# A convolution moved from layer 1's beginning into layer 0's last image, and a reordered first image

## The chip, the cores and the metric

The kernel runs on one core of one Trainium2 chip. The metric is the device time of one execution in microseconds; three executions of the kernel before took 8372.44, 8380.8 and 8384.7 us, so its median is 8380.8 us. The engines are called as in the profile: PE (matrix multiply), PEld (its weight load), DVE (vector), ACT (activation), POOL (GpSimd), SP (the queue that issues all DMAs here).

## The reference

Two layers work on 16 images of 128 channels and 56 x 56 pixels, in float32. Layer 0 is an attention block over windows, layer 1 a convolution, a state-space scan and a group norm. Cut to what matters here:

```python
# layer 0, for each image
x = x + dwconv3x3(x, pos_w, pos_b)                 # "position": 9 taps per channel
y = layernorm(x) over channels
q, k, v = split(y @ qkv_w + qkv_b)                 # 49 windows of 64 pixels
idx = top4(mean(q per window) @ mean(k per window).T)
o = softmax(q k[idx]) v[idx]  per window, 4 heads
o = o + dwconv5x5(v)                               # "lepe": 25 taps per channel
x = x + o @ wo + b
x = x + gelu(layernorm(x) @ w1 + b1) @ w2 + b2     # "MLP"
# layer 1, for each image
y = conv3x3(x, conv_w) + conv_b                    # full 128 x 128 channels, 9 taps
out = mamba(y as sequences of 8 tokens of 16)
return x + silu(groupnorm(out))
```

## The kernel before

**Layer 0** (`layer0`, L163) holds one image in a padded tile `xpad` (58 x 58 per channel, channels on the 128 partitions) and cuts it into seven blocks of eight lines, 448 pixels each, which are called rows here. For the first image everything up to the routing is done in one stretch ahead of the loop: for each row, DVE computes the nine position taps (`begin`, L246, then eight times L252), PE centres the row over the channels (L268, into the PSUM bank `g0`), ACT squares it, PE averages (L276), ACT makes the inverse deviation (L280, L281), DVE multiplies (`windows`, L289) and sums, and PE projects it to q, k and v (L303, into the banks `pvt`, `po` and `g0`), from where ACT copies them out. The next row's centring uses the bank `g0` too. Then the sums of all windows are routed (`sums`, `route`), the first five windows are gathered (`gather`, four DMAs a window on SP's queue), POOL lays three rows of v into padded tiles (`surround`), DVE does 56 slots of the local convolution (`convolve_on(56)`, which are 44 taps, as the slots of two rows alternate and the odd ones of the first 25 are empty), and POOL does the first two rows of image 1 (`beside`: a start, and seven products and sums, L262 and L264; the ninth tap is DVE's).

The loop then takes 49 windows per image (`step`). A step t issues on PE the scores of window t, the attention product of window t-2, the transposes of the weights of t-1 and, in even columns, of the values; DVE takes the largest score (L364) ahead of ACT's exponentials, which free the scores' bank for the next step, and works on taps of the local convolution; POOL scales the weights. The column c = t mod 7 decides which further matmul comes in (`piece`): in columns 1 to 3 the output product, the centring and the variance of the row before (they use `pvt` and `g0`), in columns 0, 1, 4, 5 and 6 those of the next image. In the last image there is no next one, and these latter places stay empty. `mlp` (L604) follows with the MLP of seven rows, whose results are stored to DRAM (`x1`) by one DMA per row; row 6 of an image is done within the next image, and for the last image behind the loop. At t = 46 and 48 the image after next is loaded into `xpad`.

Inside `layer0` the order of every engine and of the DMA queue is the order in which the Python code issues (`_chain` adds a dependence from each instruction to the one before it on its engine). The preparation ahead of it (constants, their scaling) is left to the scheduler. SP's queue keeps at most eight DMAs under way: the ninth waits for the first one's semaphore.

**Layer 1** (`layer1`, L713) loads its own weights once layer 0's memory is free, folds two of them with factors on DVE (L762), clears a padded tile `x1pad`, loads image 0 into it from `x1`, and convolves its seven rows one after the other into one bank (`convolve`, L782: nine taps of a 128 x 128 x 448 matmul, two passes each, then two or three ACT copies, L797). Then it loads image 1 and begins the loop over groups; each group is a row of an image. The convolution of the next image's rows is spread over the loop, so only image 0's stands ahead of it. The first group begins with the transposes of `y` (`sequences`, L830), the inner projection (L838), the rate (L851), and so on to the first DVE instruction of the scan (L937).

Of the kernel before, what the change touches and what calls it, by code (L numbers as in the profile page):

```python
# [10 lines left out]
F32 = mybir.dt.float32  # L11
U32 = mybir.dt.uint32
AF = mybir.ActivationFunctionType
# [4 lines left out]
P = 128  # L18
H = W = 56
HW = H * W  # L20
# [3 lines left out]
BLK = 448  # L24
# [114 lines left out]
def _load(nc, pool, ap, name):  # L139
    t = pool.tile(list(ap.shape), F32, tag=name, name=name)  # L140
    nc.sync.dma_start(t, ap)
    return t
# [16 lines left out]
        last[i.engine] = i.name  # L159


@with_exitstack
def layer0(ctx: ExitStack, tc: tile.TileContext, x, t, x1):  # L163

# [17 lines left out]
    w6 = ctx.enter_context(tc.tile_pool(name="l0w6", bufs=AHEAD + 1))  # L184
    banks = ctx.enter_context(tc.tile_pool(name="l0p", bufs=1, space=PSUM))

    pos = _load(nc, cst, t["a_pos"], "pos")
    lep = _load(nc, cst, t["a_lepe"], "lep")
    wqkv = _load(nc, cst, t["a_qkv"], "wqkv")
# [4 lines left out]
    ident = _load(nc, cst, t["k_ident"], "ident0")  # L194
    mean = _load(nc, cst, t["k_mean"], "mean")
    centre = _load(nc, cst, t["k_centre"], "centre")
    pos_b, ln1_g, ln1_b, lepe_b, wo_b, ln2_g, ln2_b, mlp_b2 = (vec[:, i : i + 1] for i in range(8))

    def bank(name):
# [21 lines left out]
    zero = cst.tile([P, 1], F32, tag="zero0", name="zero0")  # L221
    nc.vector.memset(zero, 0.0)

    xpad = cst.tile([P, H + 2, W + 2], F32, tag="xpad", name="xpad")
    nc.gpsimd.memset(xpad, 0.0)
    vpads = [cst.tile([P, 12, W + 4], F32, tag=f"vpad{k}", name=f"vpad{k}") for k in range(3)]
    for v in vpads:
        nc.gpsimd.memset(v, 0.0)
# [293 lines left out]
    def step(im, nxt, t):  # L522
        r, c = divmod(t, WIN)
        b = im["b"]
        n = f"{b}_{t}"
        out, row = (im, r - 1) if r else (images[b - 1], NBLK - 1)
        old, new = r > 0 or b > 0, nxt is not None
        if t + AHEAD < NW:
            gather(im, t + AHEAD)
        if t in (46, 48) and b + 2 < NB:  # L530
            load(b + 2, t // 2 - 23)

        if c < 3 and new and r:
            keep(nxt, r - 1, c)
        if c == 2 and old:
            residual(out, row)
        if c == 3 and old:
            squared(n)
        if c == 4 and old:
            deviation(n)  # L540
        if c == 5 and new:
            squared(n)
        if c == 6 and new:
            deviation(n)
        if t > 0 or b == 0:
            open_step(im, t)
        if t > 1:
            attend(im, t - 2)
        if c == 1 and r:
            collect(im, r - 1)  # L550
        if c == 4 and old:
            second(out, row)
        if c == 6 and new:
            windows(nxt, r)
        convolve_on(TAPS[c] - 1)
        if new:
            if t == 1:
                position(nxt, 1, (8,))
            if t in (10, 19, 28, 37, 45):
                position(nxt, 2 + (10, 19, 28, 37, 45).index(t), (8,))  # L560
            count = len(OPS)
            for k in range(5 * count * t // 45, min(5 * count * (t + 1) // 45, 5 * count)):
                beside(nxt, 2 + k // count, k % count)
        exponentials(im, t)
        inverse(im, t)
        if t in (1, 8, 17, 27):
            surround(im, 3 + (1, 8, 17, 27).index(t))
        if t in (36, 44) and new:
            surround(nxt, (t - 36) // 8)
        weights(im, t)  # L570
        if c == 1 and new and r:
            project(g0, 2)
        waits = c in (1, 4, 6)
        if not waits:
            piece(im, nxt, out, row, c, r)
        if t > 0:
            transpose_weights(im, t - 1)
            keep_weights(im, t - 1)
        if c % 2 == 0:
            transpose_values(im, t)  # L580
            keep_values(im, t)
        convolve_on(1)
        if waits:
            piece(im, nxt, out, row, c, r)

    def piece(im, nxt, out, row, c, r):

        old, new = r > 0 or im["b"] > 0, nxt is not None
        if c == 0 and new and r:
            project(g0, 1)  # L590
        if c == 1 and old:
            project_out(pvt)
        if c == 2 and old:
            centred(g0, out, row)
        if c == 3 and old:
            variance(pvt)
        if c == 4 and new:
            centred(g0, nxt, r)
        if c == 5 and new:
            variance(pvt)  # L600
        if c == 6 and new:
            project(g0, 0)

    def mlp(im, nxt):  # L604

# [8 lines left out]
        for m in range(count + 1):  # L614
# [10 lines left out]
            if m == 0:  # L625
                transpose_weights(im, NW - 1)
                keep_weights(im, NW - 1)
                if nxt:
                    for s in (1, 2):
                        project(g0, s)  # L630
                        keep(nxt, last, s)
                convolve_on(10)
                if nxt:
                    surround(nxt, 2)
            if m < count:
                expand(*blocks[m], 2)
            if m == 1 and nxt:
# [15 lines left out]
        _act_set(tc, EXP_LN)  # L653

    start = len(nc.cur_bb.bb.instructions)
    load(0, 0)
    load(0, 1)
    _act_set(tc, EXP_LN)
    im = images[0]
    begin(im, 0, nc.vector)  # L660
    position(im, 0, range(1, 9))
    for i in range(NBLK):
        n = f"0_{i}"
        centred(g0, im, i)
        squared(n)
        variance(ptt)
        deviation(n)
        if i + 1 < NBLK:
            begin(im, i + 1, nc.vector)
            position(im, i + 1, range(1, 9))  # L670
        windows(im, i)
        for s, at in enumerate((pvt, po, g0)):
            project(at, s)
            keep(im, i, s)
    if NB > 1:
# [3 lines left out]
    route(im)  # L679
    for w in range(AHEAD):  # L680
        gather(im, w)
    for r in range(3):
        surround(im, r)
    convolve_on(56)
    if NB > 1:
        for i in range(2):
            for k in range(len(OPS)):
# [22 lines left out]


@with_exitstack
def layer1(ctx: ExitStack, tc: tile.TileContext, x1, t, out):  # L713

# [23 lines left out]
    ps_x = ctx.enter_context(tc.tile_pool(name="l1px", bufs=1, space=PSUM))  # L740
    ps_q = ctx.enter_context(tc.tile_pool(name="l1pq", bufs=1, space=PSUM))

    conv = _load(nc, cst, t["b_conv"], "conv")
    wx = _load(nc, cst, t["b_wx"], "wx")
    wz = _load(nc, cst, t["b_wz"], "wz")
    wv = _load(nc, cst, t["b_wv"], "wv")
# [1 line left out]
    adec = _load(nc, cst, t["b_alog"], "adec")  # L748
    mask = _load(nc, cst, t["k_amask"], "amask")
    wo = _load(nc, cst, t["b_wo"], "wo1")  # L750
    vec = _load(nc, cst, t["b_vec"], "vec1")
    ident = _load(nc, cst, t["k_ident"], "ident1")
    gmask = _load(nc, cst, t["k_gmask"], "gmask")
    sel = _load(nc, cst, t["k_sel"], "sel")
    cbm = _load(nc, cst, t["k_cbm"], "cbm")
    conv_b, gn_w, gn_b, c1_b, d_w, dt_b = (vec[:, i : i + 1] for i in range(6))


    for w, name in ((wx, "b_kx"), (wv, "b_dtw")):
# [9 lines left out]
    neg = cst.tile([P, 1], F32, tag="neg", name="neg")  # L769
    nc.vector.memset(neg, -1.0)  # L770

    pad = cst.tile([P, H + 2, W + 2], F32, tag="x1pad", name="x1pad")
    nc.gpsimd.memset(pad, 0.0)
    y = cst.tile([P, HW - 64], F32, tag="y", name="y")
    pq = [ps_q.tile([P, 512], F32, tag=f"q{k}", name=f"pq{k}") for k in range(2)]
    tails = {}

    def load_image(b):
        nc.sync.dma_start(pad[:, 1 : H + 1, 1 : W + 1], x1[b].rearrange("c (h w) -> c h w", w=W))
        tails[b] = w2.tile([P, 64], F32, tag="tail", name=f"tail_{b}")  # L780

    def convolve(b, i, taps):  # L782

        tail = tails[b]
        pc = pq[0][:, 0:BLK]
        for k in taps:
            dy, dx = divmod(k, 3)
            nc.tensor.matmul(  # L788
                pc, lhsT=conv[:, k, :], rhs=pad[:, 8 * i + dy : 8 * i + dy + 8, dx : dx + W],
                start=(k == 0), stop=(k == 8),  # L790
            )
        if taps[-1] < 8:
            return
        at = i * BLK

        def put(dst, rows, src):
            nc.scalar.activation(dst[rows], pc[rows, src], AF.Identity, bias=conv_b[rows])  # L797

        lo, hi = slice(0, 64), slice(64, P)
        if i == NBLK - 1:  # L800
            put(y[:, at : HW - 64], lo, slice(0, BLK - 64))
            put(tail, lo, slice(BLK - 64, BLK))
        else:
            put(y[:, at : at + BLK], lo, slice(0, BLK))
        if i == 0:
            put(tail, hi, slice(0, 64))
            put(y[:, 0 : BLK - 64], hi, slice(64, BLK))
        else:
            put(y[:, at - 64 : at + BLK - 64], hi, slice(0, BLK))

    groups = [{"n": f"{b}_{g}", "b": b, "g": g} for b in range(NB) for g in range(NBLK)]

# [263 lines left out]
    def work(i, k):  # L1076
# [95 lines left out]
            taps = {5: (0, 1), 6: (2, 3), 7: (4,), 8: (5, 6), 9: (7, 8)}[k]  # L1172
            pe.append(partial(convolve, p["b"] + 1, p["g"], taps))
        if p and p["g"] == NBLK - 1 and k == 11 and p["b"] + 2 < NB:
            load_image(p["b"] + 2)
        if two and two["g"] == NBLK - 1 and k == 2:
            pe.append(partial(group_mean, two["b"], 0))
        if far:
# [15 lines left out]
        return (groups[i], k // 2, k % 2) if i < len(groups) else None  # L1194

    start = len(nc.cur_bb.bb.instructions)
    load_image(0)
    for i in range(NBLK):
        convolve(0, i, range(9))
    if NB > 1:  # L1200
        load_image(1)
    for i in range(-2, len(groups) + 7):
        for k in range(14):
            now = 0 <= i < len(groups)
# [22 lines left out]
@with_exitstack  # L1227
def network(ctx: ExitStack, tc: tile.TileContext, t, out):
    NB = out.shape[0]
    dram = ctx.enter_context(tc.tile_pool(name="dram", bufs=1, space=bass.MemoryType.DRAM))  # L1230
    x1 = [dram.tile([P, HW], F32, tag=f"x1_{b}", name=f"x1_{b}") for b in range(NB)]
    layer0(tc, t["x"], t, x1)
    layer1(tc, x1, t, out)


# [25 lines left out]
```

## Time and profile before

| | us |
|---|---|
| median of three runs | 8380.8 |
| the profiled execution | 8386.68 |
| its span, first to last instruction | 8384.7 |
| PE busy | 7889.6 (94%) |
| DVE busy | 7747.0 (92%) |
| POOL busy | 7036.3 (84%) |
| ACT busy | 5662.9 (68%) |
| from the start to step 0's first weights on POOL | 127.2 |
| DVE idle between the layers | 95.5 |

Busy time is the time in which an engine has an instruction in work. A matmul's end is modelled, so a busy PE need not be at its peak. Behind an instruction the timeline gives in brackets how long its engine was idle before it and what ended that: `[19.18 <-DMA x1pad<-x]` is 19.18 us of idle time, ended by the landing of a DMA from x to x1pad. Names are written out<-in. "x18" means eighteen instructions of one kind merged in one line, from the first one's start to the last one's end. The clock granted to PE was 0.983 of its full speed on average.

### The profile page before, as it was taken

What the parts mean: (1) busy time and instruction counts of PE and PEld (TensorE: products, weight loads), DVE (VectorE), ACT (ScalarE), POOL (GpSimd) and SP (SyncE); (2) the same over time, 40 slices, a digit from 0 to 9 for tenths busy, and PEclk for the clock granted to TensorE, in tenths of its full rate; (3) what the DMA queues carried; (4) which work ended last, traced back from release to release, by engine and by line L of the source; (5) the groups of instructions that cost most, each with busy time, mean ns of one, the idle gap of its engine ahead of it and who ended that gap; (6) DMA issues with size and microseconds to landing.
All of it is one profiled execution on the core that took longest, in us unless ns stands there. A gap on an engine that the chain in (4) does not pass through costs nothing.

```text
span 8384.7 us, 151590 instructions
## 1 busy us (share of the span) xinstructions
PE 7889.6 (94%) x52860; PEld 3323.8 (40%) x52860; DVE 7747.0 (92%) x10358; ACT 5662.9 (68%) x10598; POOL 7036.3 (84%) x5664
## 2 busy tenths in 40 slices
PE   6999999999999987999999999999999999999997
PEld 2444444444444443333333333333333333333332
DVE  7999999999999874999999999999999999999997
ACT  4777767777777654666666666666666666666665
POOL 5888888888887724899999999999999989999987
PEclk8999999999999998999999999999999999999998
DMA  2333333333333222334334334334334333343333
GB/s 60 86 86 87 86 89 87 87 87 87 87 88 88 75 74 70 85 92 105 92 94 107 86 96 108 83 103 108 83 103 103 87 101 102 88 104 102 88 90 81
DMA packets 764424, 757.86 MB, mean 90 GB/s; under 512 B 188688, under 2 KB 663952, under 8 KB 761616
## 3 DMA queue, kind: packets, MB, share of 16 engines
q1 hardware_dynamic: 763664, 748.18, 34.7%
q8 instruction: 422, 6.91, 0.4%
q14 instruction: 338, 2.77, 0.1%
HBM read 439.61 MB, written 102.76 MB: 65 GB/s over the span
## 4 chain that ended last, share of the span: by engine, by line
DVE 40%; POOL 24%; PE 18%; issue 11%; ACT 7%; DMA 1%; SPq 0%; POOLq 0%; ACTq 0%; DVEq 0%
DVE h L937 11%; DVE a L947 10%; DVE h L948 6%; POOL cst L952 5%; POOL xh L264 4%; POOL e L380 4%; DVE lepe L461 4%; PE a L919 4%; POOL tap L262 3%; PE x L930 2%; POOL dtx L871 2%; PE pq L788 2%; DVE sst L364 2%; PE pq L961 2%; DVE ud L906 2%
## 5 line engine op out<-in xcount | busy, mean ns | idle before, releaser
L952 POOL TENSOR_TENSOR cst<-h,cb 128x1792 f32<-128x1792 f32 x784 | 3129.4, 3998 | 374.8 <-DVE h L948 301.2
L922 ACT ACTIVATE a<-a 128x896 f32<-128x896 f32 x1568 | 1416.4, 903 | 1119.0 <-PE x L930 681.5
L937 DVE TENSOR_TENSOR h<-x,bb 128x896 f32<-128x896 f32 x1568 | 1697.7, 1083 | 164.0 <-PE x L930 123.7
L461 DVE SCALAR_TENSOR_TENSOR lepe<-vpad,lep,lepe 128x448 f32<-128x448 f32 x2688 | 1718.7, 679 | 0.6
L930 PE MATMUL x<-dtx,amask 32*128 32x448 f32 x6272 | 1618.5, 592 | 32.5 <-DVE h L937 24.9
L919 PE MATMUL a<-dt,adec 32*128 32x448 f32 x6272 | 1615.6, 591 | 35.4 <-DVE h L948 15.9
L948 DVE TENSOR_TENSOR h<-a,h 128x896 f32<-128x896 f32 x1344 | 1467.0, 1092 | 45.8
L947 DVE TENSOR_TENSOR a<-a,h 128x896 f32<-128x896 f32 x1344 | 1465.5, 1090 | 6.0 <-ACT a L922 6.0
L380 POOL TENSOR_SCALAR e<-e,sst,zero 128x256 f32<-128x256 f32 x1568 | 861.3, 559 | 454.9 <-DVE sst L376 390.7
L370 ACT ACTIVATE e<-ps,sst 128x256 f32<-128x256 f32 x1568 | 729.6, 470 | 543.0 <-DVE sst L364 488.1
L788 PE MATMUL pq<-x1pad,conv 128*128 128x448 f32 x2016 | 886.5, 559 | 27.5 <-DMA x1pad<-x 19.2
L919 PEld LDWEIGHTS a<-dt,adec 32*128 32x128 f32 x6272 | 472.4, 184 | 1050.7 <-DVE h L948 469.1
L264 POOL TENSOR_TENSOR xh<-xh,tap 128x448 f32<-128x448 f32 x735 | 841.8, 1145 | 42.6
L961 PE MATMUL pq<-cst,sel 128*32 128x448 f32 x6272 | 730.4, 551 | 1.0 <-POOL cst L952 1.0
L146 ACT ACT_TABLE_LOAD x491 | 630.0, 1283 | 9.5 <-PEq L1252 0.7
L402 PE MATMUL ptt<-ident,e 128*128 128x128 f32 x3136 | 545.6, 285 | 92.3 <-POOL e L380 74.5
L930 PEld LDWEIGHTS x<-dtx,amask 32*128 32x128 f32 x6272 | 473.3, 184 | 398.8 <-DVE h L937 378.2
L364 DVE TENSOR_REDUCE sst<-ps 128x2 f32<-128x512 f32 x784 | 540.6, 690 | 88.7 <-PE ps L358 67.1
L358 PE MATMUL ps<-sel,q 32*64 32x256 f32 x6272 | 540.2, 413 | 70.9 <-ACT e L370 64.0
L262 POOL TENSOR_SCALAR tap<-xpad,pos,zero 128x448 f32<-128x448 f32 x735 | 532.3, 724 | 34.4
L402 PEld LDWEIGHTS ptt<-ident,e 128*128 128x128 f32 x3136 | 367.0, 142 | 417.7 <-POOL e L380 240.7
L788 PEld LDWEIGHTS pq<-x1pad,conv 128*128 128x128 f32 x2016 | 348.6, 190 | 412.9 <-issue 392.6
(163 smaller groups left out, 12116.2 us busy)
## 6 DMA issues: line engine op xcount, KB each, us to landing
sel<-kv SPq DMA_DIRECT2D x3136, 64.0 KB
bb<-db SPq DMA_DIRECT2D x336, 448.0 KB
cb<-dc SPq DMA_DIRECT2D x336, 448.0 KB
xpad<-x SPq DMA_DIRECT2D x32, 784.0 KB
x<-r SPq DMA_DIRECT2D x112, 224.0 KB
x1pad<-x SPq DMA_DIRECT2D x16, 1568.0 KB
db<-bs SPq DMA_DIRECT2D x112, 224.0 KB
dc<-cs SPq DMA_DIRECT2D x112, 224.0 KB
```

The lines of the kernel that those rows point to most:

```text
L264: nc.gpsimd.tensor_add(im["xh"][i], im["xh"][i], held["tap"])
L380: nc.gpsimd.tensor_scalar(e, e, im["st", w][:, 2, p : p + 1], zero, ALU.mult, ALU.add)
L402: nc.tensor.transpose(ptt[:, P * (2 * p + h) : P * (2 * p + h + 1)], e[:, h * P : (h + 1) * P], ident)
L461: nc.vector.scalar_tensor_tensor(out, src, lep[:, k : k + 1], acc, ALU.mult, ALU.add)
L788: nc.tensor.matmul(pc, lhsT=conv[:, k, :], rhs=pad[:, 8 * i + dy : 8 * i + dy + 8, dx : dx + W], start=(k == 0), stop=(k == 8),)
L919: nc.tensor.matmul(a[:, k, :], lhsT=adec[rows, l4, :], rhs=p["dt"][rows, h, :], start=True, stop=True)
L922: nc.scalar.activation(p["a", l, jp], p["a", l, jp], AF.Exp)
L930: nc.tensor.matmul(x[:, k, :], lhsT=mask[rows, l4, :], rhs=p["dtx"][rows, h, :], start=True, stop=True)
L937: nc.vector.tensor_mul(p["h", l][:, own(jp), :], px["x"], weight)
L947: nc.vector.tensor_mul(a, a, before)
L948: nc.vector.tensor_add(p["h", l][:, own(jp), :], a, p["h", l][:, own(jp), :])
L952: nc.gpsimd.tensor_mul(c, p["h", l], p["gate", 1, l].unsqueeze(1).to_broadcast([P, 4, BLK]))
```

## The change

It has three parts.

1. **The convolution of layer 1's image 0 moves into layer 0's last image.** A class `Convolution` holds the padded tile (which is now layer 0's `xpad` as well), `y`, the weights and the biases. Its weights are loaded at the kernel's beginning. At t = 0 of the last image `conv.load(0)` brings x1[0] into the padded tile; the taps of row r are issued in the columns 5 (three taps), 6 (two), 0 (three) and 1 (one, then the ACT copies), into the bank `g0`; the last four taps of row 6 stand in `mlp`, block 0. Layer 1 starts with its loop; the load of image 1 is issued ahead of it.
2. **The image first.** Only the four edges of the padded tile are cleared, and image 0's two halves are issued ahead of all weights.
3. **The first image's rows.** POOL computes rows 5 and 6 (without their ninth tap); the centring and squaring of row i+1 are issued ahead of the multiplication of row i, in banks that alternate (`g0` and one of the lepe banks); the third projection goes to `ps`; three times eight slots of the local convolution move in between rows 4, 5 and 6, and 32 stay behind the routing.

```diff
+class Convolution:
+    def __init__(self, nc, pool, t, x1):
+        self.nc, self.t, self.x1, self.tails = nc, t, x1, {}
+        self.pad = pool.tile([P, H + 2, W + 2], F32, tag="pad", name="pad")
...
+    def load(self, b):
+        self.nc.sync.dma_start(self.pad[:, 1 : H + 1, 1 : W + 1], self.x1[b].rearrange("c (h w) -> c h w", w=W))
+
+    def taps(self, bank, i, taps):
+        for k in taps:
+            dy, dx = divmod(k, 3)
+            self.nc.tensor.matmul(
+                bank[:, 0:BLK], lhsT=self.weights[:, k, :],
+                rhs=self.pad[:, 8 * i + dy : 8 * i + dy + 8, dx : dx + W], start=(k == 0), stop=(k == 8),
+            )
...
+    xpad = conv.pad
+    for edge in (xpad[:, 0, :], xpad[:, H + 1, :], xpad[:, :, 0], xpad[:, :, W + 1]):
+        nc.gpsimd.memset(edge, 0.0)
+    for two in range(2):
+        nc.sync.dma_start(xpad[64 * two : 64 * two + 64, 1 : H + 1, 1 : W + 1], xv[0, two])
     pos = _load(nc, cst, t["a_pos"], "pos")
...
+    conv.bring()
...
-    xpad = cst.tile([P, H + 2, W + 2], F32, tag="xpad", name="xpad")
-    nc.gpsimd.memset(xpad, 0.0)
...
+        if t == 0 and early and not new:
+            conv.load(0)
...
+        if early and not new:
+            first(r if c > 4 else r - 1, {5: (0, 1, 2), 6: (3, 4), 0: (5, 6, 7), 1: (8,)}.get(c, ()))
...
+    early = NB > 2
+    def first(i, taps):
+        if i >= 0 and taps:
+            conv.taps(g0, i, taps)
+            if taps[-1] == 8:
+                conv.keep(g0, 0, i)
...
+                elif early:
+                    first(last, range(5, 9))
...
-    load(0, 0)
-    load(0, 1)
...
+    means = {}
+    def norm_begun(i):
+        centred((g0, sums_[1])[i % 2], im, i)
+        means[i] = held["pc"]
+        squared(f"0_{i}")
+    for i in (NBLK - 2, NBLK - 1):
+        for k in range(len(OPS)):
+            beside(im, i, k)
     begin(im, 0, nc.vector)
     position(im, 0, range(1, 9))
+    norm_begun(0)
     for i in range(NBLK):
-        n = f"0_{i}"
-        centred(g0, im, i)
-        squared(n)
         variance(ptt)
-        deviation(n)
-        if i + 1 < NBLK:
+        deviation(f"0_{i}")
+        if i + 1 < NBLK - 2:
             begin(im, i + 1, nc.vector)
             position(im, i + 1, range(1, 9))
+            norm_begun(i + 1)
+        elif i + 1 < NBLK:
+            position(im, i + 1, (8,))
+            norm_begun(i + 1)
+        if i == NBLK - 3:
+            surround(im, 0)
+            surround(im, 1)
+        if i >= NBLK - 3:
+            convolve_on(8)
+        held["pc"] = means[i]
         windows(im, i)
-        for s, at in enumerate((pvt, po, g0)):
+        for s, at in enumerate((pvt, po, ps[:, 0, :])):
...
-    for r in range(3):
-        surround(im, r)
-    convolve_on(56)
+    surround(im, 2)
+    convolve_on(32)
...
-    conv = _load(nc, cst, t["b_conv"], "conv")
...
-    pad = cst.tile([P, H + 2, W + 2], F32, tag="x1pad", name="x1pad")
-    nc.gpsimd.memset(pad, 0.0)
...
-    load_image(0)
-    for i in range(NBLK):
-        convolve(0, i, range(9))
+    if NB < 3:
+        conv.load(0)
+        for i in range(NBLK):
+            convolve(0, i, range(9))
     if NB > 1:
-        load_image(1)
+        conv.load(1)
```

## The prediction

> **What bounds the kernel.** I read the page first, then the chain of waits and the stretches by time, then the timeline where a stretch was thin. On the page all 40 slices but a few show PE and DVE at 9 tenths; the chain of waits is DVE 40%, POOL 24%, PE 18%. The steady stages, which the change does not touch, are full. The change touches three places: the start (0 to 127 us), layer 0's last image (2947 to 3144), and the hand-over to layer 1 (3144 to 3250).
>
> The hand-over, from the timeline (start, length, engine, line, out<-in):
>
> ```profile
> 3144.69 0.32 SPq L500 DMA_DIRECT2D x<-r  x1
> ...
> 3163.11 9.60 PE L788 MATMUL pq<-x1pad,conv 128*128 128x448 f32 x18 [19.18 <-DMA x1pad<-x]
> 3174.23 7.03 PE L788 MATMUL pq<-x1pad,conv 128*128 128x448 f32 x18 [1.51 <-ACT y L797]
> ...
> 3216.21 7.03 PE L788 MATMUL pq<-x1pad,conv 128*128 128x448 f32 x18 [1.36 <-ACT y L797]
> 3224.76 0.66 PE L830 MATMUL pq<-ident,y 128*128 128x128 f32 x4 [1.51 <-ACT y L797]
> 3226.04 3.05 PE L838 MATMUL pq<-seq,wx 128*128 128x448 f32 x4 [0.62 <-ACT seq L832]
> ```
>
> Layer 0 issues its last store at 3144.69, an image is loaded until 3163, seven rows of convolution run alone, and only at 3224.76 does layer 1's first group begin. DVE waits 95.5 us here, nothing beside it. That is the prize: 3226.04 - 3144.69 = 81.35 us from store to first projection.
>
> The start, from the timeline:
>
> ```profile
> 88.07 0.62 DVE L289 TENSOR_TENSOR y<-g,rstd 128x448 f32<-128x448 f32 x1 [6.65 <-ACT rstd L281]
> 91.58 0.72 POOL L246 TENSOR_SCALAR xh<-xpad,pos,vec 128x448 f32<-128x448 f32 x1 [23.99 <-DMA xpad<-x]
> ...
> 121.26 0.72 POOL L246 TENSOR_SCALAR xh<-xpad,pos,vec 128x448 f32<-128x448 f32 x1
> 124.57 0.69 DVE L364 TENSOR_REDUCE sst<-ps 128x2 f32<-128x512 f32 x1
> ...
> 127.20 1.10 POOL L380 TENSOR_SCALAR e<-e,sst,zero 128x256 f32<-128x256 f32 x2 [5.22 <-DVE sst L376]
> ```
>
> The last norm (y, row 6) is at 88.07; POOL gets image 1 at 91.58 and works 29.7 us on its two rows; step 0 starts at DVE's reduce, 124.57, behind 44 local-convolution taps, and POOL's first weights come at 127.20. I measure the start by that 127.20.
>
> **Hand-over: what goes.** The load of image 0, the memset and the convolution leave. What is late next is layer 1's weights. They are issued after the last store, 0.47 us apart; b_kx is now twelfth, so it issues 0.4 + 11 x 0.47 = 5.6 us after the store and lands about 2.4 us later (1.06 MB; at 245 to 362 GB/s, the rates of 3145 to 3150, that is 3 to 4 us of transfer). The fold on DVE takes 0.43 (L762), so the first projection comes 8.6 us after the store, not 81.35: **-72.7 us**. b_dtw now waits for that fold (one buffer) and is ready 11 us after the store; it is needed at the rate matmul, 2.84 us after the first projection, so it fits. The load of image 1 moves ahead of all this, to the SP queue's place between the last gathers and the output stores; its 10.8 us lie beside the last MLP. The stores behind it have three buffers at 4.5 us per block, so they bear it. Ends: 70 to 74.
>
> **Last image: what comes.** 63 taps, each two passes of 0.376 us (7.03 us / 18, plus the tail), 47.4 us of PE, and 16 small evacuations on ACT. Stretches of the last image and of the one before (us, then busy by engine, granted clock, DMA):
>
> ```profile
> 2950.00:3097.00 147.00, 119.95 (x1464) 66.01 (x1460) 123.33 (x243) 95.49 (x289) 56.87 (x109) 0.93 0.29 82
> 2760.00:2909.00 149.00, 136.24 (x1518) 72.88 (x1522) 137.34 (x266) 116.47 (x325) 124.73 (x187) 0.98 0.29 81
> ```
>
> PE is 82% busy, so the taps don't fit. I follow the order on PE. A step holds the next scores until exp has read the bank: 2.61 us from reduce to reduce at the least. PE's own work in a step is scores 0.6, attention 0.43, weight transposes 0.6, value transposes 0.64 (column 6: 0.32; odd columns none), a 0.75 product in columns 1, 2, 3. With the taps: column 5 0.6+0.43+2.26+0.6 = 3.9 against a spacing of 2.61 now: +1.25; column 6 (two taps) 3.45 against 2.62: +0.83; column 0 (three) 4.5 against 3.03: +1.47; column 1 (one tap behind the output product) +0.75; column 2, whose centring matmul shares bank g0 and must wait for two evacuations of 0.64, +0.5. Seven rows have columns 5 and 6, six the others: 8.8 + 5.8 + 8.8 + 4.5 + 3.0 = 30.9. The last four taps, 3.0 us, stand in the MLP at a place where PE now idles 0.76: +2.5 to 3. Sum **+34 us**. Another way: 119.95 + 47.4 = 167.4, at the 91% of the image before (136.24/149) is 183: +36. Ends: as cheap as the next image's five products per row are (rows of 21.5 with them, 20.4 without, so 1.1 us for 3.76 of work): 14; wholly exposed with its evacuations: 51. The load of image 0 (10.8 us) is queued between gathers: the gather behind it is needed five steps, about 14 us, later, so it is hidden; a gap of that size would cost once what exceeds 14. Net of both: 72.7 - 34 = **-38.7 us**.
>
> **The start, where a rule and bare durations part.** Image first: the vector of biases becomes the ninth DMA, behind the image (SP keeps eight out), and row 0's first instruction needs both. Before, all was landed at 19.23; now only ident, mean and centre (0.2 MB) come later: 17.5. But in the built order of DVE the five bias instructions stand behind that first instruction and wait for the bias matmuls: 2 x 1.42 on PE + 1.3 on DVE + hand-overs = 4.3. So taps begin at 21.8, two later than the old 19.77: no gain there.
>
> Then two rows go to POOL (15 us each, 91.58 to 106.43), beside DVE's rows 0 to 4. By bare durations a row is 6.24 on DVE plus 1.3 for the norm, so the fourth norm comes at 56, the others follow at the chain's pace, and the start shortens by some 19 us. Against it stands the Trainium skill's page "SBUF — State Buffer", section "Who interferes with whom": a DVE instruction with two SBUF inputs and a GpSimd instruction that reads SBUF exclude each other for whole instructions. The position taps (L252: xpad and xh) are of that kind; the lepe taps, which accumulate in PSUM, are not. The trace agrees, row by row:
>
> ```profile
> 242.01 1.14 POOL L264 TENSOR_TENSOR xh<-xh,tap 128x448 f32<-128x448 f32 x1
> ...
> 242.29 1.34 DVE L252 SCALAR_TENSOR_TENSOR xh<-xpad,pos,xh 128x448 f32<-128x448 f32 x1
> ...
> 312.51 1.28 POOL L262 TENSOR_SCALAR tap<-xpad,pos,zero 128x448 f32<-128x448 f32 x1
> 312.52 0.68 DVE L252 SCALAR_TENSOR_TENSOR xh<-xpad,pos,xh 128x448 f32<-128x448 f32 x1
> ```
>
> 0.68 becomes 1.34 behind a POOL instruction (it ends 0.48 after POOL's), 0.72 becomes 1.28 behind a DVE one (POOL restarts 0.13 before DVE's end). In turns, a POOL pair of 0.72 + 1.14 takes 0.72 + 1.14 + 2 x 0.354 = 2.57 us and lets two taps through: 1.28 a tap, not 0.716 (5.73 for eight at 19.77). POOL's 14 pairs then last until about 54. DVE: row 0 from 21.8 to 32.1, row 1 to 42.9, norm, row 2 to 55, norm, rows 3 and 4 alone: the fourth norm at 70.7 (62.86 before). Rows 4 to 6 run at the chain: projections, variance, two activations, 5.5 us at PE's fast matmul (0.92 to 1.02 a pair) and 8.5 at its slow one (1.70 to 1.86), without the centring and square, which the alternating banks put ahead; I take 7: the last norm at 92, four later than before. But 12 of the 44 lepe taps are then done: 92 + 8.1 (as 88.07 to 96.19) + 32 x 0.6 + 0.7 = 120 for step 0's reduce. POOL: xpad's last reader is row 6's ninth tap, behind the fifth norm, 79.7; load 13.1 (78.4 to 91.5 now), two rows 29.7: 122.5 against 127.2. **-4.7 us** by the rule, -19 by bare durations; as rows of this trace show the rule, I take it. Ends: +4 (slow matmuls, late vector) to -19.
>
> **Sum.** -38.7 - 4.7 = -43.4. The profiled execution took 8386.7 (span 8384.7) and would come to 8343; the median of the three runs is 5.9 under it, so **8337 us**.
>
> **Rivals.** 0.2% is 17 us, about what a measurement tells from no change.
> - **Taps wholly exposed** (PE's 82% and the lumps of three taps speak for it, the 2.61 floor against): 51, so -21.7 - 4.7 = -26: 8354. Chance 0.13.
> - **Both halves cheap** (POOL and DVE share better than those rows, or the taps hide like the next image's products): -57 to -63, 8318 to 8324. Chance 0.18.
> - **Slower: PE's granted clock.** The last image shows 0.93 and the hand-over 0.82; if the added load pulls it down, every matmul in the row stretches. PE's sum is 23.2 us a row at full clock; the loss reaches the 77 us saved when seven rows take 31.4 each, at a mean clock near 0.74; at half clock rows of 46 us lose 180 and the kernel ends near 8484. Rows as loaded as this stand at 0.98 in the image before. Chance 0.03.
> - **The convolution is not hidden at all** because the load waits: it is ordered behind an old reader only; 0.02, near 8375.
> The forecast's own case has 0.64. Faster 0.94, same 0.03, slower 0.03; the range of 8312 to 8358 takes in the second rival and most of the first.
>
> **What would show it.** Right: DVE's idle at the hand-over near 23 us in place of 95.5; L830 some 7 us after the last store; reduces of the last image spaced 3.9, 3.5, 4.5, 3.8 in columns 5, 6, 0, 1; position taps of rows 0 to 2 near 1.3 us, POOL's two rows ending near 54; image 1 in POOL near 92. Wrong: taps near 0.7 beside POOL (start much shorter), rows of the last image at 22 or at 27.5 us, a DMA wait on sel in its first steps, or b_kx late.

## The result and the profile after

The changed kernel takes **8320.7 us** (median of four runs, 8319.0 to 8322.9) against 8376.8 for the kernel before (four runs, 8372.4 to 8384.7): a ratio of 0.9932 with a 95% interval of 0.9915 to 0.9949, so 56 us less, 43 to 71. In five later runs it took 8325.9 beside 8375.8: 0.9941 (0.9927 to 0.9954), 50 us less. The forecast was 8337 us, in a range of 8312 to 8358. The profiled execution of after took 8321.0 (span 8319.0), that of before 8386.7, so these two differ by 65.7 us. Stage by stage, with the spans of the two profiles:

| stage | before, us | after, us | difference | forecast |
|---|---|---|---|---|
| start of the span to the last image's first reduce | 2946.81 | 2936.08 | -10.7 | -4.7 |
| last image, first to last reduce | 147.89 | 167.83 | +19.9 | +30.9 |
| last reduce to layer 0's last store | 49.99 | 50.53 | +0.5 | +2.5 to 3 |
| last store to layer 1's first projection | 81.35 | 8.50 | -72.9 | -72.7 |
| first projection to the end | 5158.65 | 5156.01 | -2.6 | 0 |

At the end of image 0 the lead is 7.9 us, not 10.7; the other 2.9, and the last line's 2.6, come from stages whose code is the same in both. Most of the 2.9 is before's own: in images 12 to 14 its profiled execution loses 1.0 to 4.0 us against every other kernel here. More on that below.

The hand-over of after, from the timeline (start, length, engine, line, operation, out<-in, then idle time and what ended it):

```profile
3154.44 0.32 SPq L551 DMA_DIRECT2D x<-r  x1
...
3160.07 0.43 SPq L843 DMA_DIRECT2D b_kx<-b_kx  x1
...
3160.76 1.08 PE L884 MATMUL pq<-ident,y 128*128 128x128 f32 x4 [7.07 <-DMA ident<-k_ident]
...
3162.37 0.42 DVE L844 TENSOR_TENSOR wx<-wx,b_kx 128x256 f32<-128x256 f32 x1
...
3162.94 3.32 PE L892 MATMUL pq<-seq,wx 128*128 128x448 f32 x4 [1.10 <-DVE wx L844]
```

The convolution and its load are gone from here. The factor b_kx is issued 5.6 us after the store, the fold (L844) starts 2.3 later, and the projection follows at 8.50. DVE's idle time ahead of layer 1's first product fell from 95.51 us to 22.53. On the page, the idle time of that line over the whole kernel fell accordingly, from 164.0 to:

```profile
L991 DVE TENSOR_TENSOR h<-x,bb 128x896 f32<-128x896 f32 x1568 | 1696.0, 1082 | 91.0 <-PE x L984 51.2
```

The start of after, from the timelines of DVE and POOL:

```profile
19.71 9.72 DVE L303 SCALAR_TENSOR_TENSOR xh<-pad,pos,xh 128x448 f32<-128x448 f32 x8
...
22.52 1.37 POOL L315 TENSOR_TENSOR xh<-xh,tap 128x448 f32<-128x448 f32 x1
23.99 0.97 POOL L313 TENSOR_SCALAR tap<-pad,pos,zero 128x448 f32<-128x448 f32 x1
...
84.62 0.62 DVE L340 TENSOR_TENSOR y<-g,rstd 128x448 f32<-128x448 f32 x1 [1.22 <-ACT rstd L332]
...
89.60 0.72 POOL L297 TENSOR_SCALAR xh<-pad,pos,vec 128x448 f32<-128x448 f32 x1 [16.53 <-DMA pad<-x]
...
109.88 0.68 DVE L415 TENSOR_REDUCE sst<-ps 128x2 f32<-128x512 f32 x1
...
119.94 0.68 DVE L303 SCALAR_TENSOR_TENSOR xh<-pad,pos,xh 128x448 f32<-128x448 f32 x1 [5.76 <-POOL xh L315]
...
121.03 1.09 POOL L431 TENSOR_SCALAR e<-e,sst,zero 128x256 f32<-128x256 f32 x2
```

Read it from the end. POOL's first weights come at 121.03, not 127.20. Step 0's reduce is 14.7 us earlier than before (124.57), but DVE then waits 5.76 us in step 1 for POOL's row 1 of image 1, and the weights stand behind that row. So of the 14.7, 6.2 are left at the weights. (Seven profiled executions have this start; their first weights come at 120.35 to 122.34, so 4.9 to 6.9 earlier than the one execution of before.) In the first lines, eight position taps of 0.716 each take 9.72 us while POOL works, 1.2 a tap, and POOL's own pair has grown from 0.72 + 1.13 to 0.97 + 1.37.

The last image: intervals between DVE's successive reduces in row 2 (us), the columns in order of execution. The last two lines belong to experiments below:

| | c0 | c1 | c2 | c3 | c4 | c5 | c6 | row |
|---|---|---|---|---|---|---|---|---|
| before | 3.03 | 3.10 | 2.83 | 2.65 | 3.48 | 2.61 | 2.61 | 20.3 |
| forecast | 4.5 | 3.8 | 3.3 | | | 3.9 | 3.5 | |
| after | 4.34 | 3.85 | 3.30 | 2.64 | 3.49 | **3.23** | 3.44 | 24.3 |
| each tap twice | 6.59 | 4.61 | 3.29 | 2.64 | 3.49 | 5.49 | 4.94 | 31.1 |
| taps from column 4 on | 4.34 | 3.86 | 3.29 | 2.65 | 4.30 | 3.11 | 2.68 | 24.2 |

### The profile page after: what moved, and what is told of

Same layout as the page of the kernel before. It is cut to its first block, busy times and chain, and to the rows that moved or that the text cites. A ratio compares the mean times of both kernels' runs of the same rounds, so it can differ in the third digit from the quotient of the medians.

```text
span 8319.0 us, 151598 instructions
## 1 busy us (share of the span) xinstructions
PE 7858.1 (94%) x52860; PEld 3316.4 (40%) x52860; DVE 7746.6 (93%) x10342; ACT 5659.3 (68%) x10598; POOL 7064.8 (85%) x5696
## 4 chain that ended last, share of the span: by engine, by line
DVE 39%; POOL 25%; PE 18%; issue 10%; ACT 7%; DMA 1%; SPq 0%; POOLq 0%; ACTq 0%; DVEq 0%
DVE h L991 11%; DVE a L1001 10%; DVE h L1002 6%; POOL cst L1006 5%; POOL xh L315 5%; POOL e L431 4%; PE a L973 4%; POOL tap L313 3%; DVE lepe L512 3%; PE x L984 2%; POOL dtx L925 2%; DVE sst L415 2%; PE pq L1015 2%; DVE ud L960 2%; PE pq L184 1%
## 5 line engine op out<-in xcount | busy, mean ns | idle before, releaser
L315 POOL TENSOR_TENSOR xh<-xh,tap 128x448 f32<-128x448 f32 x749 | 859.4, 1147 | 43.7
L184 PE MATMUL pq<-pad,conv 128*128 128x448 f32 x1890 | 834.7, 559 | 0.0
L313 POOL TENSOR_SCALAR tap<-pad,pos,zero 128x448 f32<-128x448 f32 x749 | 548.7, 733 | 35.7
L459 ACT COPY att<-ptt 128x512 f32<-128x512 f32 x784 | 458.6, 585 | 73.7 <-PE ptt L453 65.8
```

The source lines that it names most:

```text
L184: self.nc.tensor.matmul(bank[:, 0:BLK], lhsT=self.weights[:, k, :], rhs=self.pad[:, 8 * i + dy : 8 * i + dy + 8, dx : dx + W], start=(k == ...
L315: nc.gpsimd.tensor_add(im["xh"][i], im["xh"][i], held["tap"])
```

## The experiments

Totals of one kernel spread over some 20 us (the kernel before: 8367 to 8390 in 25 runs). Most verdicts below are therefore read from stages of the trace, which repeat much better: the last image of the nine runs with the change's order of taps takes 167.4 to 168.4 us in all of them.

### The halves alone

The changed kernel with the old start put back (`e1_middle`: the `load` calls behind the weights, the loop of before, one bank):

```diff
-    for i in (NBLK - 2, NBLK - 1):
-        for k in range(len(OPS)):
-            beside(im, i, k)
...
-        for s, at in enumerate((pvt, po, ps[:, 0, :])):
+        for s, at in enumerate((pvt, po, g0)):
```

> The change with the old start put back: image after the weights, all seven rows on VectorE, one bank for the means; the convolution of layer 1's first image still lies inside layer 0's last. Theory (the middle gives some 52 us and the start some 8): 8325, about 52 us below before; the first POOL weights at about 127 us as in before, and the hand-over from the last store to the first projection of layer 1 8.5 us. Rival (the parts need each other: the steadier lead of the new start is what keeps POOL and the transfers of the later images in step): less than 45 us below before.

Measured: 42 us below before (0.9948, 0.9931 to 0.9965, so 29 to 58). The hand-over is 8.57 us and the last image 167.65, as in after; the first weights come at 129.04, 1.8 later than before. 42 lies under the rival's bound of 45, but the theory's 52 lies within the interval too, so the total can't tell. The stages speak for the theory: the two that the move touches are the same with either start. The lead over before, -0.2 us at the end of image 0, is +2.4 at the start of image 8 and +5.2 at the last image; after's goes from 7.9 to 10.7, so the old start loses nothing on the way.

The other half (`e2_start`: the new start, the convolution where it was):

```diff
-    early = NB > 2
+    early = False
...
-    if NB < 3:
+    if NB > 0:
         conv.load(0)
```

> Only the new start; the convolution of layer 1's first image stays between the layers, as in before. Theory: 7 to 9 us below before, 8368 to 8370, with the first POOL weights at 121 us and every later step of image 0 7.7 us ahead of before, since GpSimd's own chain (rows 5 and 6 of image 0, then rows 0 and 1 of image 1) sets the first weights. Rival (the 15 us by which step 0's reduce comes earlier carry through): 13 to 15 us. Third possibility: the last image's start is not the middle's affair at all but the lead grows from 7.9 to 10.7 us over the images, then 10 to 11 us.

Measured: 20 us below before (0.9974, 0.9963 to 0.9984, so 13 to 31). **This missed on the high side of all three expectations.** The start is near what was expected: first weights at 120.35, the later steps 8.4 to 8.9 us ahead. The surplus stands at the hand-over: 60.4 us from the last store to the first projection, where before has 81.35. The convolution is still there, but it begins at once.

To see whether the start has to do with it, one kernel keeps the old start and the old place of the convolution, and has only the shared buffers and their early loads (`e12_loads`, the edits of the last two diffs together).

> Neither the new start nor the moved convolution: only the convolution's weights, the vector and the pad's zero edge come at the beginning of the kernel, as in the changed one, and the rest is as in before. Theory (of the hand-over's 81 us some 21 are loads that need nothing of layer 0 and a memset, 60 are the image's convolution itself): 60.4 us from the last store to the first projection, as the kernel with only the new start had it, so 21 us below before. Rival (that kernel's 21 us came from its other start): nothing below before.

Measured: 17 us below before (0.9981, 0.9974 to 0.9987, so 11 to 22). Its timeline at the hand-over:

```profile
3140.51 0.32 SPq L549 DMA_DIRECT2D x<-r  x1
3140.53 7.03 PE L184 MATMUL pq<-pad,conv 128*128 128x448 f32 x18 [0.78 <-DVE r L548]
...
3200.88 2.66 PE L873 MATMUL pq<-seq,wx 128*128 128x448 f32 x4 [0.62 <-ACT seq L867]
```

60.37 us, and the first tap 0.02 us after the store; before, it waited 19.18 us for the image. In this kernel the padded tile lives outside both layers, so the load had no memory to wait for: it is issued at 2903.61, behind the tile's last readers (the last image's position taps), and lies under some 230 us of other work. So 21 of the hand-over's 72.9 us are won by the shared buffers and their early loads alone: 18.4 by the earlier first tap, and 2.6 because the first 18 matmuls take 7.03 in place of 9.60 (at a granted clock of 1.00 over 3140 to 3150; before has 0.76 over 3163 to 3174). The computation's move won the other 52. But it costs 25.2 in the last image against this kernel (142.68 there), so its own gain is some 26 us, not much more than that of the buffers; the totals of this kernel and of `e1_middle`, 17 and 42 below before, show the same. The start pays 3.8 us here at the first weights (130.96) and 2.1 to 2.5 at the later steps; 21 less these is the measured 17 to within its interval.

### What a tap costs

Each tap of the moved convolution issued twice, which doubles the first image's convolution sum (`e5_taps_twice`):

```diff
-            conv.taps(g0, i, taps)
+            for tap_ in taps:
+                for again in range(2):
+                    conv.one(g0, i, tap_, tap_ == 0 and again == 0, tap_ == 8 and again == 1)
```

> Each tap of the moved convolution is issued twice on TensorE, inside columns 5, 6, 0 and 1 of the last image's rows (which doubles that image's sum and is not what layer 1 should get). Nine taps at 0.37 to 0.42 us are 3.4 to 3.8 us a row; the changed kernel's typical row is 24.28 against 20.32 before. Theory A (TensorE is what every step waits for in these columns, and the small first slack is used up): each second tap is exposed wholly, rows of about 27.9, the last image some 25 us longer than the changed kernel's 167.8. Theory B (the taps' cost is a hand-over between engines, paid once for a column): rows of 25 or less, under 6 us more in all.

Measured: rows of 31.05, 6.77 more than after's, and 210.4 us for the last image, 42.5 more. Theory A holds in kind, but not in its size: it said rows of 27.9 and 25 us for the image, as its text prices a tap too low. Each tap is two passes of 0.376, 0.75 us, and 9 x 0.75 = 6.77. In the table, columns 5, 6, 0 and 1 grow by 2.26, 1.50, 2.25 and 0.76, which is 3, 2, 3 and 1 taps at 0.75. In PE's timeline (c5 with its six taps, then c6 with its four):

```profile
2986.27 4.78 PE L191 MATMUL g<-pad,conv 128*128 128x448 f32 x12
2991.42 0.68 PE L416 MATMUL ps<-sel,q 32*64 32x256 f32 x8
2993.25 3.18 PE L191 MATMUL g<-pad,conv 128*128 128x448 f32 x8
2996.36 0.68 PE L416 MATMUL ps<-sel,q 32*64 32x256 f32 x8
```

So the second nine taps are wholly exposed, while the first nine, just as long, cost 3.97 us a row: PE had 2.8 us a row of slack, and the change has used up all of it. The granted clock doesn't fall under this load: it is 0.99 in both. Stretches of after and of this kernel (busy time of PE, PEld, DVE, ACT, POOL with counts, then granted clock, DMA share, GB/s):

```profile
2940.00:3100.00 160.00, 145.58 (x1526) 80.51 (x1530) 119.93 (x235) 100.90 (x290) 54.67 (x105) 0.99 0.32 85
```

```profile
2940.00:3140.00 200.00, 185.77 (x1622) 100.45 (x1614) 120.11 (x235) 100.04 (x288) 54.00 (x104) 0.99 0.26 68
```

It even rises with the taps. Row 1 of the last image has a granted clock of 0.88 in the three profiled executions without taps in it (before, `e2_start`, `e12_loads`) and 1.00 in the eleven with them. Over the whole image it is 0.94 in before and 0.99 in after.

Next, two taps moved up into column 4 (`e6_column_4`):

```diff
-            first(r if c > 4 else r - 1, {5: (0, 1, 2), 6: (3, 4), 0: (5, 6, 7), 1: (8,)}.get(c, ()))
+            first(r if c > 3 else r - 1, {4: (0, 1), 5: (2, 3), 6: (4,), 0: (5, 6, 7), 1: (8,)}.get(c, ()))
```

> The nine taps spread over columns 4, 5, 6, 0 and 1 (2, 2, 1, 3, 1) in place of columns 5, 6, 0 and 1 (3, 2, 3, 1). Theory A (column 5 can take one of its three taps for nothing because VectorE is 0.6 us late there, and column 4 has the same spare time, since VectorE's second norm of the row before holds its reduce): column 4's interval stays 3.5 or grows to 4.1, 5 falls from 3.23 to about 2.6, 6 from 3.43 to about 2.9: 0.3 to 1.2 us a row, 2 to 8 us in all. Theory B (the taps of column 4 must wait for their bank, which VectorE's second norm of that column reads last): column 4 grows to 4.5 or more and the row is as long or longer.

Measured: rows of 24.23 against 24.28; the image is 1.5 us longer, as the first row takes 26.51 against 25.43 and the last, of six intervals, 21.54 against 20.85. Neither theory. Column 4 pays 0.8 for its two taps, column 6 gives back 0.76, column 5 0.12, and the row is the same. The first line below is from row 0, the second from row 2:

```profile
2955.84 1.74 PE L184 MATMUL g<-pad,conv 128*128 128x448 f32 x4 [1.77 <-DMA pad<-x]
...
3004.41 1.77 PE L184 MATMUL g<-pad,conv 128*128 128x448 f32 x4 [0.32 <-DVE y L532]
```

In row 0 the taps come a step earlier and wait 1.77 us for the image. In row 2 PE waits 0.32 us for DVE's second norm, which reads the bank, so the bank plays a small part. What is hidden is the same in both orders: of the taps in columns 4 and 5, 1.63 us a row in after and 1.69 here, of those in column 6, 0.67 and 0.68. In these columns it doesn't matter, as far as this one variant shows, from which the taps take PE's slack.

Last, the load of the first image left out (`e7_no_load`):

```diff
-        if t == 0 and early and not new:
-            conv.load(0)
```

> The load of layer 1's first image into the pad is left out, so the moved convolution works on the last image of layer 0's input. Theory: the 1.6 MB load lies wholly beside the last image's first steps: rows 0 to 6 the same within 0.3 us each. Rival (the load delays the gathers of the first row): row 0 falls from 25.43 to 22 to 23, as 20.85 plus the taps of two columns would have it, and the last image by 2 to 3 us.

Measured: row 0 25.10 against 25.43, rows 1 to 6 the same within 0.01, the image 167.51 against 167.83. The load is hidden but for the 0.26 us that PE waits for it in after's row 0 (1.02 in `e3_dve_rows`, nothing in seven other kernels with this order of taps). Row 0's length is not its doing.

### What the start is worth

All seven rows of image 0 on DVE (`e3_dve_rows`):

```diff
-    for i in (NBLK - 2, NBLK - 1):
-        for k in range(len(OPS)):
-            beside(im, i, k)
...
-        if i + 1 < NBLK - 2:
+        if i + 1 < NBLK:
```

> The new start, but rows 5 and 6 of image 0 go to VectorE like the others and GpSimd has nothing to do before image 1's rows. Theory A (the two engines shut each other out while both read SBUF; and GpSimd's chain, not VectorE's, sets the first weights): taps back from 9.7 to 5.7 to 6.2 us for eight; last norm at about 78 instead of 84.6; image 1's rows on GpSimd begin before 89.6, first POOL weights at about 117, some 4 us below the changed kernel. Theory B (the GpSimd rows are a help: they take 11 us of taps off VectorE): step 0's reduce later than 109.9 and the weights later than 121.0, the kernel 3 to 8 us slower than the changed one.

Measured: 8319.0 in its one run; the start, from the timelines of DVE and POOL:

```profile
19.39 5.79 DVE L303 SCALAR_TENSOR_TENSOR xh<-pad,pos,xh 128x448 f32<-128x448 f32 x8
...
85.85 0.71 POOL L297 TENSOR_SCALAR xh<-pad,pos,vec 128x448 f32<-128x448 f32 x1 [26.37 <-DMA pad<-x]
...
116.05 0.68 DVE L303 SCALAR_TENSOR_TENSOR xh<-pad,pos,xh 128x448 f32<-128x448 f32 x1 [3.70 <-POOL xh L315]
...
117.14 1.09 POOL L431 TENSOR_SCALAR e<-e,sst,zero 128x256 f32<-128x256 f32 x2
```

Theory A. The total can't tell a few us in one run; the stages can. The same eight taps take 5.79 us in place of 9.72; the last norm is at 82.05 (84.62), image 1's load is issued at 72.45 in place of 76.04, and the weights come 3.9 us earlier than in after (3.2 to 5.2 against the seven executions above), the later steps 2.5. The last norm was expected at 78: row 6 waits 2.9 us for its deviation, behind the chain of projections. The two rows on GpSimd are a loss. DVE's 24 taps of rows 0 to 2 take 29.2 us beside POOL in place of 17.6, about what the two rows would take on DVE (14 taps and two starts, 11 us); and what ends last at the start is the pad: its last reader releases image 1's load, and that releases POOL's two rows.

The weights loaded ahead of the image, as before (`e4_weights_first`: the image's two loads moved behind `centre`, ahead of `conv.bring()`).

> The changed kernel with the image's load put back behind the weights' loads. Theory: image first is worth at most 2 us: the taps of the changed kernel begin at 19.71 us and those of before at 19.77; with the weights first they begin at 19.7 to 20.5, GpSimd's rows begin at about 19 instead of 15.9 and end at 56 instead of 52.8, and the first POOL weights come 0 to 3 us later. Rival (image first is what the start's gain rests on): first POOL weights 5 us or more later, at 126 or later.

Measured: the first taps start at 19.89 against 19.71, GpSimd's rows run from 19.51 to 56.1 against 15.85 to 52.8, the weights come at 121.71, 0.7 later than in after, the later steps 2.4 to 2.6 later. The weights' time lies within the 120.35 to 122.34 of the kernels with the image first, so no gain shows there; their later steps are 6.1 to 8.9 us ahead of before, 5.2 to 5.6 here. As the theory has it: image first is worth at most some 3 us.

### A version that beats both

The hand-over's rest is SP's queue, as the fence of after shows. So wx, b_kx and the decays were loaded in the last image, and the unit matrix was kept from layer 0 (`e8_resident`):

```diff
+        self.held = {
+            n: pool.tile(list(t[n].shape), F32, tag=n, name=n) for n in ("k_ident", "b_wx", "b_kx", "b_alog")
+        }
...
             conv.load(0)
+            conv.hold(("b_wx", "b_kx", "b_alog"))
...
-    wx = _load(nc, cst, t["b_wx"], "wx")
+    wx, adec = conv.held["b_wx"], conv.held["b_alog"]
```

> What is left of the hand-over (8.5 us from the last store to layer 1's first projection): wx, its factor b_kx and the decays are loaded during the last image, the unit matrix is layer 0's own, and wv and its factor are first in the queue. Theory (SyncE's queue is what ends last: the unit matrix is the eighth load and the factor the twelfth, 0.47 us apart, 2.3 us from issue to landing): the first transposes 0.5 to 1 us after the store, the first projection 3 to 4 us after it, 4.5 to 5.5 us less, and the same at the first inject. Rival (ScalarE's table loads and the copy before the projection, or the gate's transfers, hold it): less than 2 us at the first inject.

Measured: 8309.4 in its one run. The hand-over, from the timeline:

```profile
3154.82 0.32 SPq L559 DMA_DIRECT2D x<-r  x1
3154.84 0.66 PE L891 MATMUL pq<-k_ident,y 128*128 128x128 f32 x4 [0.78 <-DVE r L558]
...
3156.25 1.77 PE L899 MATMUL pq<-seq,b_wx 128*128 128x448 f32 x4 [0.75 <-ACT seq L893]
```

1.43 us in place of 8.50, more than the theory had, since no factor has to be waited for at all. The first inject (DVE's first product of the scan) comes 24.3 us after the store, against 32.0 to 33.1 in the eight runs with the change's hand-over: 8 us. Part of it is speed: the same four matmuls take 1.77 here and 3.32 in after, behind 7 us of idle PE.

Then it was joined with the seven rows on DVE (`e9_both`), and in a further kernel row 1 of image 1 was shared between the engines (`e10_shared_row`), beside the changed kernel once more (`e11_after`):

```diff
-            for k in range(len(OPS)):
+            for k in range(len(OPS) if i == 0 else 9):
                 beside(images[1], i, k)
         position(images[1], 0, (8,))
+        position(images[1], 1, range(5, 8))
```

> Two findings in one kernel: all seven rows of image 0 on VectorE (no GpSimd rows), and layer 1's first weights resident, as in the runs before. Theory (the two places are independent): 2.5 us from the start and 4 to 12 us from the hand-over, 6 to 14 us below the changed kernel run beside it. Rival (the residence's 11.9 us was mostly a lucky run, 4 us of it shown by the first inject): 6 us or less below.

> As the one before, and row 1 of image 1 is shared: GpSimd forms its first five taps, VectorE the next three, instead of all eight on GpSimd. Theory (GpSimd's chain of rows 0 and 1, 31 us, sets the first weights, while VectorE then waits 3.7 us for it in step 1): first weights at about 113 to 114 instead of 117, and 2 to 3 us less at the later steps. Rival (VectorE's own chain of local taps sets the later steps): step 5's reduce the same within 1 us.

> The changed kernel itself, on the same chip and in the same rounds as the two combined ones: about 55 us below before, between the two profiled results of 56 and 46 to 65.

Measured, all in the same rounds: 8315.0 with both, 8310.0 with the shared row, 8325.9 for the changed kernel, 8375.8 before. The first is 10.9 below the changed kernel, as the stages have it (2.0 at the start against after's profile, 2.7 against this run's, and 8 at the hand-over). The last is **0.9923 of before (0.9910 to 0.9937)**, 66 us less, and 16 below the changed kernel; its stages show 4.4 to 5.1 at the start and 8 at the hand-over, 12 to 13 in all; the other 3 us lie within the spread of the runs. Its timeline shows what the sharing does:

```profile
110.13 2.30 DVE L311 SCALAR_TENSOR_TENSOR xh<-pad,pos,xh 128x448 f32<-128x448 f32 x3 [3.86 <-POOL xh L323]
112.34 0.68 DVE L423 TENSOR_REDUCE sst<-ps 128x2 f32<-128x512 f32 x1
...
114.97 1.09 POOL L439 TENSOR_SCALAR e<-e,sst,zero 128x256 f32<-128x256 f32 x2 [3.73 <-DVE sst L435]
```

Step 0's reduce is later than in after (112.34 against 109.88), the weights 6 us earlier, and now POOL waits for DVE, where DVE waited for POOL. The weights were expected at 113 to 114: DVE's three taps wait 3.86 us for POOL's last sum.

## The prediction, step by step

**The hand-over** was right, to 0.2 us in 72.7: b_kx, not the convolution, is late next, issued 5.6 us after the store as worked out, and DVE's idle is 22.53 where 23 was said. What the prediction didn't separate is that 21 us of this need no computation to be moved.

**The last image** was right in kind, an exposed cost on PE, and too dear: 30.9 for the columns against 19.9 in these two profiles. **The step that failed is column 5's**, "3.9 against a spacing of 2.61 now: +1.25". The 3.9 is right; it is PE's spacing from scores to scores. The 2.61 is DVE's spacing from reduce to reduce, and the two are not the same thing in this column. Before, DVE and PE in columns 4 to 6 of row 2, from the two engines' timelines:

```profile
3005.14 0.62 DVE L481 TENSOR_TENSOR y<-g,rstd 128x448 f32<-128x448 f32 x1 [0.42 <-ACT rstd L281]
...
3007.51 0.69 DVE L364 TENSOR_REDUCE sst<-ps 128x2 f32<-128x512 f32 x1
...
3010.12 0.69 DVE L364 TENSOR_REDUCE sst<-ps 128x2 f32<-128x512 f32 x1
```

```profile
3006.07 0.68 PE L358 MATMUL ps<-sel,q 32*64 32x256 f32 x8 [0.57 <-ACT e L370]
...
3009.30 0.68 PE L358 MATMUL ps<-sel,q 32*64 32x256 f32 x8 [0.59 <-ACT e L370]
```

and after, on PE:

```profile
3002.11 0.68 PE L409 MATMUL ps<-sel,q 32*64 32x256 f32 x8 [0.57 <-ACT e L421]
...
3003.08 2.52 PE L184 MATMUL g<-pad,conv 128*128 128x448 f32 x6
...
3005.97 0.68 PE L409 MATMUL ps<-sel,q 32*64 32x256 f32 x8
```

A reduce normally starts 0.82 us after its scores (3009.30 to 3010.12). In column 5 it starts 1.44 after them (3006.07 to 3007.51), because DVE is still busy with the second norm and the taps behind it. So PE's spacing there was already 3.23, and the three taps stretch it to 3.86: +0.63 a row, 4.4 us less over seven rows. Columns 6, 1 and 2 came out at 0.83, 0.75 and 0.47 a row as forecast (0.83, 0.75, 0.5), column 0 at 1.31 in place of 1.47. Added up over the intervals between the first and the last reduce, with column 6 in six rows, this gives 4.4 + 5.0 + 7.9 + 4.5 + 2.8 = 24.6. The last 4.7 down to 19.9 are not in the columns: before's profiled execution was slow in its last image. PE waited 3.6 us there for gathers, in rows 5 and 6, and the granted clock was low: row 0 took 24.27 us at 0.86, and 22.46 at 1.00 in the kernel with the loads alone, which has the same instructions there. In that kernel the image takes 142.68 without the taps, not 147.89, so against it they cost 25.2.

**The MLP's four taps** cost 2.3 at the first blocks, close to the forecast, but the last row's MLP took 5.5 us from its norm to its residual in place of 7.2, its first matmul pairs at 1.02 and 0.91 in place of 1.74 and 1.70. That is TensorE's clock, below, and not the change: 1.7 us of luck.

**The start**: the choice of the exclusion over bare durations was right, 1.19 to 1.24 us a tap (1.28 said), POOL's rows ending at 52.8 (54), and the kernel without POOL's rows shows the taps back at 0.72. The times worked out for DVE were too late by 2 to 10 us: taps from 19.71 (21.8), the last norm at 84.62 (92), step 0's reduce at 109.88 (120). The last two norms follow in 5.3 us each, where 7 was taken, which is about half of the last norm's 7.4. That this hardly reached the sum has one reason, which the prediction had: it measured by POOL, and POOL's chain from the pad's last reader ends last (121.03; 122.5 said). -6.2 came at the weights and -7.9 at the steps behind, for -4.7.

**The rivals.** Wholly exposed taps (8354) fell by the rows of 24.3, though a second set of taps is wholly exposed. The clock rival (8484) fell: 0.99 over the last image, even with twice the taps. The unhidden convolution fell at the hand-over's 8.5 us. The cheap halves (8318 to 8324) gave the right total, by another sum than their own: POOL and DVE share no better than the rows said, and the taps cost 4.0 us a row, not the 2 that the next image's products would suggest. That the total came out there is luck.

The total is 16 us under the forecast: 6.3 too dear in the last image's columns by the clean rows, 2 in the MLP, 3 in the start. Another 4 lie in the base: the forecast counts from 8380.8, the median of three runs of before, and with the fourth it is 8376.8. The last 1 is within the spread of the runs. Where that spread arises can be seen in part: from the first inject to the end, stages with one and the same code took 5128 to 5143 us in the fourteen profiled executions. These times go with TensorE's mean granted clock over that stretch: 5127.8 and 5129.3 at 0.988 in `e8_resident` and `e1_middle`, 5139.9 and 5143.2 at 0.984 in `e11_after` and `e10_shared_row`; over all fourteen the correlation is -0.89. Why one execution is granted more than another was not tried.

## What to carry to other kernels

Take a step's old and new spacing on the same engine: where an engine has had work of its own between its release and its next instruction, another engine's delay up to that amount is free. When work is moved over a boundary, ask first what only its buffers and loads would give; 21 of 73 us here were had by a tile that outlives the layer. And help from GpSimd beside DVE instructions with two SBUF inputs is to be counted as turns, not as parallel work; follow what its last read releases.

## What had not been expected of the hardware

TensorE's granted clock falls in short thin places, not under load. Behind 7 us of idle time at the hand-over of after the four projection matmuls took 3.32 us at a granted clock of 0.64 (3161 to 3170); with the weights resident they took 1.77 in a stretch at 1.00. The row of the last image that holds taps at 1.00 and none at 0.88, above, is the other side of it.

The last row's MLP shows how much hangs on it. The same twelve matmuls stand there behind the same 1.99 us of idle PE in all fourteen profiled executions. In six kernels the clock is 1.00 over them and the row takes 5.5 us from norm to residual; in seven, before among them, it is 0.74 and the row takes 7.1 to 7.2; in `e5_taps_twice` it is 0.61 and 8.5. Before, then after:

```profile
3137.46 1.74 PE L491 MATMUL ps<-y,wm 128*128 128x448 f32 x2 [1.99 <-DVE y L481]
```

```profile
3148.92 1.02 PE L542 MATMUL ps<-y,wm 128*128 128x448 f32 x2 [1.99 <-DVE y L532]
```

The Trainium skill, page "TensorE: Matmul & The Clock Gate", section "Part 1: The HAM clock gate", says that the clock is halved after a window of about 3.4 us without work, and that the windows run freely. The 7 us at the hand-over agree. The last row doesn't quite: in before the clock is 1.00 over 3131.0 to 3137.5 and 0.50 over 3137.6 to 3141.0, and PE's longest idle time in the ten us ahead of that is 1.99, so a window with some work in it was enough. Freely running windows would account for the two kinds of kernels; which falls on which side was not predicted by anything here, so that part stays an inference.
